# Diagonal tiles of causal attention on a packed TensorE array: the later 64 keys of a tile start 64 queries further on

## The chip, the core and the metric

The kernel runs on one core of one Trainium2 chip. A core has TensorE (PE in the profile; PEld are its weight loads), VectorE (DVE), ScalarE (ACT), GpSimd (POOL) and SyncE (SP), which issues most DMA transfers. Engines run side by side and wait for each other through semaphores. The metric is the device time of one execution in microseconds; the time before is the median of three runs.

## What is computed

The input is 4096 tokens of 256 numbers and a dense 4096 x 4096 adjacency matrix. A graph layer comes first (adjacency times features, divided by the degree, two linear maps, a residual). Then comes one transformer block in fp32: RMS norm, causal attention with 4 query heads and 2 key/value heads of 64, and a mixture of 8 experts with the 2 best per token. The part that matters here is:

```python
scores = jnp.einsum('bhtd,bhsd->bhts', q, k) / jnp.sqrt(jnp.float32(HD))
causal = jnp.tril(jnp.ones((Tx, Tx), dtype=bool))
scores = jnp.where(causal[None, None], scores, jnp.float32(-1e+30))
att = jax.nn.softmax(scores, axis=-1)
y = jnp.einsum('bhts,bhsd->bhtd', att, v)
```

A query t takes part only with keys s up to t. The order of the keys inside a sum does not matter, as long as scores and values use the same one.

## The kernel before

There are three stages: the graph layer (to about 508 us), attention with the routing of tokens to experts (508 to about 1017 us), and the experts. Queries are cut into 8 blocks of 512 (NB), keys into 32 tiles of 128 (four to a block, TB). Blocks are worked off in the order 3, 0, 4, 1, 5, 2, 6, 7 (ORDER). For each block `b` there are two passes `p`, each over one query head of either key/value head `j`; for each (b, p) the list `order_of(b)` (L795) names the key tiles `s`: all tiles of earlier blocks, then the block's own four, the diagonal ones, mixed with the last full tiles; the block's first own tile d0 comes last (for block 0 it is first, since it has no earlier tiles). There are 288 (b, p, s) in all, of which 64 are diagonal.

For one (b, p, s) the work is this.

- `scores` (L817). Keys stand on the output's partitions, queries along its columns: `ps[key, j, query]`. TensorE's 128 x 128 array is used as four quarters of 64 x 64. The product for key half `k` (HP = 64 keys) and head `j` contracts over 64 numbers, on the rows of the array that belong to `j`, and writes the partitions, so the columns of the array, that belong to `k`. On a diagonal tile `i` of its block the queries before the tile are left out: `off = i * 128`, so the four products are 512, 384, 256 or 128 wide. They are all equally wide.
- The exponential (L834) on ScalarE reads `ps` and writes a room `pt` of the ring `pt_all` (or of space lent by `res_all`, `qT_all`, `late`; `room_for_probs`, L756). On diagonal tiles GpSimd then zeroes the triangle above the diagonal in the first 128 columns (L836, a select over 128 partitions x 2 heads x 128 queries).
- `totals` (L843) on VectorE adds `pt` to the running sums, from which denominators are made later.
- `values` (L858) multiplies: the contraction is over the keys, so key half `k` sits on the rows of the array and head `j` on its columns. Half `k` sums into a bank of its own, `accs[b, p][k]` (named y_first, y_second, y_third in turn); `unload` adds the two banks.

The scores of five tiles are made ahead of values (LEAD = 5). Two PSUM buffers (`p_sc0`, `p_sc2`, in turn) take scores. The order on each engine is the order of the code (`manual_schedule`). The main loop (L1998) is:

```python
for m in range(scored, min(n + LEAD + (s == order_of(b)[0]) + 1, len(keys))):
    scores(*keys[m])
    ...
        totals(*keys[m - 1])
...
values(b, p, s)
if s == order_of(b)[-1]:
    unload(b, p)
if n % 2:
    place_for_steps(n // 2)
```

After every second tile (a place) other steps are put in, by `at` and `after` (L1132): denominators (L899), the output projection (`project`, L948), residual, routing (`choose`), `place` (L1039, which counts where each token goes in its expert's list, with 64x64 products of 32 columns at L1059) and scatters of token rows to lists in DRAM by GpSimd (L1109 copies one number of the latest `pt` into `gap`, L1110 is the indirect DMA). The products of `place` are written so:

```python
for r in range(2):
    some = slice(r * HP, (r + 1) * HP)
    for i, w in ((0, tri), (1, ones)):
        for h in range(2):
            ...
            nc.tensor.matmul(pls[r][to, i * n : (i + 1) * n], w[some, to], flat[0][some], ...)
```

Values `vv[b][key in tile, t, ...]` are written long before: for blocks 0 to 6 in `values_and_logits` of the graph stage (L636, one copy from PSUM for two tiles), for block 7 in `heads` (L256, one copy for each tile). Keys `kT[b]` hold 64 numbers of a head on partitions and keys along columns.

Of the kernel before, what the change touches and what calls it, by code (L numbers as in the profile page):

```python
# [12 lines left out]
AF = mybir.ActivationFunctionType  # L13
ALU = mybir.AluOpType
# [3 lines left out]
P = 128  # L18
# [3 lines left out]
TB = 4  # L22
NH, NKV, HD = 4, 2, 64
HEAD_ORDER = (0, 2, 1, 3)
NE = 8
# [35 lines left out]
] + list(range(NW - LAST, NW)) + list(range(NM, NG))  # L61
REG = N + SM
ROW = C + 1 + NE


@with_exitstack
def fast_kernel(
# [24 lines left out]
    nc = tc.nc  # L92
# [10 lines left out]
        out=tri, in_=tri, pattern=[[1, P]], compare_op=ALU.is_gt, fill=0.0,  # L103
        base=0, channel_multiplier=-1,
# [5 lines left out]
    for e in range(NE):  # L110
        nc.gpsimd.memset(run[0][:, e : e + 1], float(e * REG))
    lists = tc.dram_tile([NE * REG + SM, ROW], F32, name="lists")
    acc_dram = tc.dram_tile([N + SM, C], F32, name="acc_dram")
# [6 lines left out]
    for e in range(NE):  # L120
# [21 lines left out]
    qT = [  # L142
        qT_all[:, b * 1024 : (b + 1) * 1024].rearrange("p (c i) -> p c i", c=2)
        for b in range(NB)
    ]
# [34 lines left out]
    kT = [kvp.tile([P, 512], F32, name=f"kT{b}") for b in range(NB)]  # L180
    vv = [kvp.tile([P, TB, NKV * HD], F32, name=f"vv{b}") for b in range(NB)]
# [38 lines left out]
    def rotated(pool, b, t, hT, pj, ro, r2, cs, sn, unscale):  # L220
# [19 lines left out]
        nc.gpsimd.tensor_sub(ro[:, :, 0, :], ro[:, :, 0, :], r2[:, :, 0, :])  # L240
        nc.gpsimd.tensor_add(ro[:, :, 1, :], ro[:, :, 1, :], r2[:, :, 1, :])

    def heads(pool, b, t, hT, ro, tr):

        rof = ro.rearrange("p h s d -> p (h s d)")
        trf = tr.rearrange("p a b i -> p (a b) i")
        for c in range(2):
            nc.tensor.matmul(
                trf[:, 3, :], hT[:, c, t * P : (t + 1) * P], wqkv_sb[:, c, QK + NE :],
                start=(c == 0), stop=(c == 1),  # L250
            )
        for m in range(3):
            nc.tensor.transpose(trf[:, m, :], rof[:, m * P : (m + 1) * P], ident)
        nc.scalar.copy(qT[b][:, :, t * P : (t + 1) * P], trf[:, 0:2, :])
        nc.scalar.copy(kT[b][:, t * P : (t + 1) * P], trf[:, 2, :])
        nc.scalar.copy(vv[b][:, t, :], trf[:, 3, :])  # L256


    with (
# [20 lines left out]
        for h in range(2):  # L280
            some = slice(h * TB // 2, (h + 1) * TB // 2)
# [291 lines left out]
        def qkv(b):  # L573

            made = {}
# [49 lines left out]
            def values_and_logits():  # L625
                for h in range(2):
                    pj = p_tr.tile([P, 2, 2, P], F32, tag="tr", name=f"pv_{b}_{h}")
                    pj = pj.rearrange("p c t i -> p c (t i)")
                    for i in range(2):
                        at = (2 * h + i) * P  # L630
                        for c in range(2):
                            nc.tensor.matmul(  # L632
                                pj[:, i, 0 : NE + P], made["hT"][:, c, at : at + P],
                                wqkv_sb[:, c, QK:], start=(c == 0), stop=(c == 1),
                            )
                    nc.scalar.copy(vv[b][:, 2 * h : 2 * h + 2, :], pj[:, :, NE : NE + P])  # L636
                    for i in range(2):
                        t = 2 * h + i
                        nc.scalar.activation(
                            first_lg[b][:, t, :], pj[:, i, 0:NE], AF.Copy,  # L640
                            scale=made["ratio"][:, t],
                        )
# [84 lines left out]
    with (  # L727
# [14 lines left out]
        pt_all = sp.tile([P, 9 * 1024], F32, name="pt_all")  # L742
        KEPT = ROW - C
        LATE_XT = 2 * (NF + 1) * GR
# [38 lines left out]
        def next_bank():  # L783
            y_next[0] += 1
            return y_banks[(y_next[0] - 1) % 3]
# [9 lines left out]
        def order_of(b):  # L795

            whole, (d0, *part) = range(TB * b), range(TB * b, TB * b + TB)
            if not b:
                return [d0, *part]
            return [  # L800
                *whole[:-2], part[0], whole[-2], part[1], whole[-1], part[2], d0,
            ]
        HP = P // 2
        probs, sums, accs, ys, flats, chosen, squares, picks, narrows = ({} for _ in range(9))
        puts = []

# [7 lines left out]
        ]  # L814
        inverses = tc.dram_tile([2, NH, 512], F32, name="inverses")

        def scores(b, p, s):  # L817

            sb, i = divmod(s, TB)
            off = i * P if sb == b else 0  # L820
            w = 512 - off
            ps = next(p_sa).tile([P, 2, 512], F32, tag="sc", name=f"sc_{b}_{p}_{s}")
            for k in range(2):
                for j in range(2):
                    hd = slice(j * HD, (j + 1) * HD)
                    nc.tensor.matmul(  # L826
                        ps[k * HP : (k + 1) * HP, j, :w],
                        kT[sb][hd, i * P + k * HP : i * P + (k + 1) * HP], qT[b][hd, p, off:],
                        start=True, stop=True,
                    )  # L830
            room = room_for_probs()
            room_of[id(room)] = b, p, s
            pt = room.rearrange("p (j i) -> p j i", j=2)
            nc.scalar.activation(pt[:, :, :w], ps[:, :, :w], AF.Exp, scale=HD ** -0.5)  # L834
            if sb == b:
                nc.gpsimd.affine_select(  # L836
                    out=pt[:, :, 0:P], in_=pt[:, :, 0:P], pattern=[[0, 2], [1, P]],
                    compare_op=ALU.is_ge, fill=0.0, base=0, channel_multiplier=-1,
                )
            probs[b, p, s] = pt  # L840
            latest[:] = [pt]

# [15 lines left out]
        def values(b, p, s):  # L858
            sb, i = divmod(s, TB)
            off = i * P if sb == b else 0  # L860
            pt = probs.pop((b, p, s))
            if s == order_of(b)[0]:
                accs[b, p] = next_bank(), next_bank()
            for k in range(2):
                some = slice(k * HP, (k + 1) * HP)
                for j in range(2):
                    hd = slice(j * HD, (j + 1) * HD)
                    nc.tensor.matmul(  # L868
                        accs[b, p][k][hd, off:], vv[sb][some, i, hd], pt[some, j, : 512 - off],
                        start=(s == order_of(b)[0]), stop=(s == order_of(b)[-1]),  # L870
                    )

        def unload(b, p):
            ys[b, p] = ax.tile([P, 512], F32, tag=f"yT{p}", name=f"yT_{b}_{p}")
# [58 lines left out]
        def inputs(b):  # L933

            row = ax.tile([P, TB, ROW], F32, tag="row", name=f"row_{b}")
            for t in range(TB):
# [53 lines left out]
        def over(v):  # L990
            return v.to_broadcast([P, TB, NE])
# [47 lines left out]
        def place(b):  # L1039
# [12 lines left out]
            else:  # L1052
                pls = two_banks(f"pl_{b}")
# [4 lines that stand above are left out]
                            to = slice(h * HP, (h + 1) * HP)  # L1058
                            nc.tensor.matmul(  # L1059
# [21 lines left out]
            nc.vector.tensor_add(oh1, oh1, oh2)  # L1081
            nc.vector.tensor_mul(row[:, :, C + 1 : ROW], oh1, over(den))
            chosen[b] = slots
# [97 lines left out]
        def last_qkv():  # L1181
# [4 lines left out]
            def norm():  # L1186
                h0 = ax.tile([P, TB, ROW], F32, tag="row", name="h0_l")
                for t in range(TB):
                    nc.vector.tensor_scalar(
                        in_order(h0[:, t, 0:C]), in_groups(res[b][:, t, :]),  # L1190
                        mv[b][:, t, 0:1], both[b][:, t], op0=ALU.subtract, op1=ALU.mult,
                    )
                made["ratio"] = ratio(ax, b)
                nc.sync.dma_start(
                    turning_l.rearrange("(t p) c -> p t c", p=P), h0[:, :, 0:C]
                )
# [98 lines left out]

        pad = eg.tile([P, ROW], F32, name="pad")
        nc.gpsimd.memset(pad, 0.0)
# [5 lines left out]
        def step_iota(name, n, first, step):  # L1303
# [1522 lines left out]
```

## Time and profile before

| | us |
|---|---|
| three runs | 1511.27, 1512.95, 1515.51 |
| their median | 1512.95 |
| the profiled execution's own time | 1511.47 |
| its span, from first to last instruction | 1509.8 |
| attention stage | 508 to 1017 |
| TensorE busy over the span | 1496.9 (99%) |
| VectorE, ScalarE, GpSimd busy | 1083.9, 544.9, 568.9 |
| granted TensorE clock | 0.999 |

A line of a group reads: code line, engine, operation, output<-inputs, shapes (partitions x elements; 64*64 is the part of the array in use), count, busy us, mean ns of one, idle time before and what ended it. A line of a timeline begins with the start and the duration in us. Matmuls are pipelined, and their ends are modelled, so starts say more than durations.

### The profile page before, as it was taken

The numbers are of one execution on the slowest core, as the hardware profiler recorded it, in microseconds if no ns is written. First come the engines' busy times: TensorE is split into PE (matmuls) and PEld (weight loads), VectorE is DVE, ScalarE is ACT, GpSimd is POOL, SyncE is SP. The second block draws the span as 40 slices with busy tenths as digits, with TensorE's granted clock in tenths as the row PEclk, the third lists the DMA queues.
The fourth block names the chain that finished last, engine by engine and source line by source line (L and its number), as shares of the span: only waits on it lengthen the run. The fifth ranks groups of instructions, "written<-read, shape, count | busy, mean of one in ns | idle before, by whom it ended". The sixth has DMA issues, their size and how long they took to land. (4 is left out here: it accounts for less than half of the span.)

```text
span 1509.8 us, 28585 instructions
## 1 busy us (share of the span) xinstructions
PE 1496.9 (99%) x10731; PEld 1102.8 (73%) x10731; DVE 1083.9 (72%) x2239; ACT 544.9 (36%) x975; POOL 568.9 (38%) x649
## 2 busy tenths in 40 slices
PE   9999999999999999999999999999999999999997
PEld 7888888888888544444444444358899999999996
DVE  7855666656765577779879879795676877777872
ACT  2102011021020455655665655653222334343341
POOL 2102122121221331374565553551523464554542
PEclk9999999999999999999999999999999999999999
DMA  7435645555566000011010110029977898999965
GB/s 244 133 119 178 201 147 173 166 170 171 162 184 185 21 15 22 24 59 30 30 59 28 36 41 30 30 87 336 251 180 225 254 278 233 264 272 246 270 155 135
DMA packets 127005, 220.56 MB, mean 146 GB/s; under 512 B 79530, under 2 KB 103338, under 8 KB 113226
## 3 DMA queue, kind: packets, MB, share of 16 engines
q1 hardware_dynamic: 113322, 200.39, 42.3%
q0 software_dynamic: 12720, 17.47, 6.6%
q8 instruction: 86, 1.41, 0.4%
q10 hardware_dynamic: 816, 0.79, 0.2%
q14 instruction: 61, 0.50, 0.1%
HBM read 188.67 MB, written 31.33 MB: 146 GB/s over the span
## 5 line engine op out<-in xcount | busy, mean ns | idle before, releaser
L826 PE MATMUL sc<-qT_all,kT 64*64 64x512 f32 (+3 forms) x2304 | 282.1, 557 | 0.5 <-ACT pt_all L834 0.3
L538 PE MATMUL acc<-a,g 128*128 128x256 f32 x1024 | 244.0, 379 | 0.0
L538 PEld LDWEIGHTS acc<-a,g 128*128 128x128 f32 x1024 | 194.1, 190 | 32.2 <-issue 6.7
L826 PEld LDWEIGHTS sc<-qT_all,kT 64*64 64x64 f32 x2304 | 91.3, 133 | 128.9 <-issue 109.9
L834 ACT ACTIVATE pt_all<-sc 128x1024 f32<-128x1024 f32 (+3 forms) x157 | 149.0, 956 | 99.9 <-PE sc L826 95.6
L1917 POOL DMA_INDIRECT acc_dram<-y,late x40 | 63.3, 1583 | 177.0 <-ACT y L1906 118.9
L538 PE MATMUL acc<-more_sums,g 128*128 128x256 f32 x512 | 126.3, 379 | 0.0
L854 DVE TENSOR_TENSOR late<-late,pt_all 128x1024 f32<-128x1024 f32 (+3 forms) x92 | 106.6, 1159 | 20.4 <-ACT pt_all L834 9.0
L661 POOL TENSOR_TENSOR rot<-rot,tables 128x512 f32<-128x512 f32 x21 | 34.4, 1636 | 192.4 <-ACT rot L657 137.3
L538 PEld LDWEIGHTS acc<-more_sums,g 128*128 128x128 f32 x512 | 97.2, 190 | 13.2
L868 PE MATMUL y_second<-pt_all,vv 64*64 64x512 f32 (+3 forms) x440 | 105.0, 555 | 0.0
L868 PE MATMUL y_first<-pt_all,vv 64*64 64x512 f32 (+3 forms) x440 | 104.3, 553 | 0.0
L1837 PE MATMUL h<-late,qT_all 128*128 128x256 f32 (+1 forms) x616 | 104.0, 327 | 0.0
L1837 PEld LDWEIGHTS h<-late,qT_all 128*128 128x128 f32 x616 | 93.5, 191 | 9.6 <-ACT late L1521 0.8
L1110 POOL DMA_INDIRECT lists<-row,slots x64 | 91.3, 1426 | 17.2 <-issue 14.5
L636 ACT COPY vv<-pv 128x256 f32<-128x256 f32 x14 | 5.2, 373 | 251.9 <-PE pv L632 216.0
L868 PE MATMUL y_third<-pt_all,vv 64*64 64x512 f32 (+3 forms) x376 | 89.8, 557 | 0.0
L1844 DVE TENSOR_TENSOR late<-si,h 128x256 f32<-128x256 f32 (+2 forms) x87 | 39.3, 466 | 64.4 <-ACT si L1843 44.6
L657 ACT ACTIVATE rot<-pq 32x512 f32<-32x512 f32 x84 | 49.5, 589 | 82.5 <-DVE qT_all L655 33.1
L1843 ACT ACTIVATE si<-h 128x256 f32<-128x256 f32 (+2 forms) x87 | 36.1, 418 | 107.0 <-PE h L1837 93.1
L538 PE MATMUL acc<-qT_all,g 128*128 128x256 f32 x256 | 65.7, 379 | 0.0
L854 DVE TENSOR_TENSOR sum_all<-sum_all,pt_all 128x1024 f32<-128x1024 f32 (+3 forms) x49 | 53.5, 1093 | 15.8 <-POOL pt_all L836 9.9
(480 smaller groups left out, 3321.4 us busy)
## 6 DMA issues: line engine op xcount, KB each, us to landing
a<-in_adj_dram SPq DMA_DIRECT2D x64, 1024.0 KB
qT_all<-in_w_dram SPq DMA_DIRECT2D x18, 1408.0 KB
pt_all<-in_w_dram SPq DMA_DIRECT2D x16, 1408.0 KB
res_all<-in_w_dram SPq DMA_DIRECT2D x17, 768.0 KB
pt_all<-in_w_dram SPq DMA_DIRECT2D x16, 768.0 KB
res_all<-in_w_dram SPq DMA_DIRECT2D x8, 1408.0 KB
qT_all<-in_w_dram SPq DMA_DIRECT2D x9, 768.0 KB
late<-lists SPq DMA_DIRECT2D x96, 64.0 KB
```

What stands on the lines that cost most here:

```text
L538: nc.tensor.matmul(acc[bank][:, at, :], g[jb][:, right, k, :], m[left][:, k, :], start=(jb == 0 and k == 0 and at == 0), stop=(jb == NB - ...
L657: nc.scalar.activation(rot[n * Q : (n + 1) * Q, :], pj[(n ^ 1) * Q : ((n ^ 1) + 1) * Q, :], AF.Copy, scale=1.0 if n % 2 else -1.0,)
L661: nc.gpsimd.tensor_mul(rot, rot, tables[b][:, 1, :])
L826: nc.tensor.matmul(ps[k * HP : (k + 1) * HP, j, :w], kT[sb][hd, i * P + k * HP : i * P + (k + 1) * HP], qT[b][hd, p, off:], start=True, st ...
L834: nc.scalar.activation(pt[:, :, :w], ps[:, :, :w], AF.Exp, scale=HD ** -0.5)
L854: nc.vector.tensor_add(sums[b, p][:, :, off:], before[:, :, off:], pt[:, :, : 512 - off])
L868: nc.tensor.matmul(accs[b, p][k][hd, off:], vv[sb][some, i, hd], pt[some, j, : 512 - off], start=(s == order_of(b)[0]), stop=(s == order_o ...
L1110: put = nc.gpsimd.indirect_dma_start(out=lists[:, :], out_offset=bass.IndirectOffsetOnAxis(ap=chosen[b][:, k, t, :], axis=0), in_=flats[b] ...
L1837: nc.tensor.matmul(ps[m % 2][:, m // 2 - q, :], w13_sb[:, c, m * P : (m + 1) * P], xT[:, c, :], start=(c == 0), stop=(c == 1),)
L1843: nc.scalar.activation(si[:, 0:both, :], ps[0][:, 0:both, :], AF.Silu)
L1844: nc.vector.tensor_mul(hT[:, q : q + both, :], si[:, 0:both, :], ps[1][:, 0:both, :])
L1917: put = nc.gpsimd.indirect_dma_start(out=(acc_dram if k < NM - LAST else out)[:, :], out_offset=at, in_=y[:, h, :], in_offset=None, comput ...
```

## The change

On a diagonal tile, the first 64 queries of the tile see only its first 64 keys. The change leaves out the products of the later 64 keys with these queries.

- `narrowed(b, s)` gives, for each key half k of the layout, how many query columns are skipped: 64 for the half that holds the later keys, 0 for the other. `scores` and `values` start their products that much further on. In `values` the first tile of a sum (only block 0's d0 is diagonal there) is left whole.
- In odd tiles the halves are swapped: k = 0 holds the later 64 keys. `key_half(t, k)` picks the columns of `kT` for it, and `value_rows` writes the rows of `vv` in this order. For that, one copy of two tiles becomes one copy for the even tile and two copies of 64 rows for the odd tile; in `heads` one copy becomes two on odd tiles.
- The exponential of a diagonal tile runs on all 128 partitions from column 64 on; a second one takes columns 0 to 63 of the early half's 64 partitions. GpSimd zeroes the triangle in the early half (64 partitions, columns 0 to 63), sets columns 0 to 63 of the late half to 0 (memset), and zeroes the triangle in the late half (columns 64 to 127): three instructions for one. `totals` stays as it is.

```diff
+def key_half(t, k):
+    return slice((k ^ t % 2) * HP, ((k ^ t % 2) + 1) * HP)
...
+    def value_rows(b, t, made):
+        if t % 2 == 0:
+            nc.scalar.copy(vv[b][:, t, :], made)
+        else:
+            for k in range(2):
+                nc.scalar.copy(vv[b][k * HP : (k + 1) * HP, t, :], made[key_half(t, k)])
...
-        nc.scalar.copy(vv[b][:, t, :], trf[:, 3, :])
+        value_rows(b, t, trf[:, 3, :])
...
-                    nc.scalar.copy(vv[b][:, 2 * h : 2 * h + 2, :], pj[:, :, NE : NE + P])
+                    for i in range(2):
+                        value_rows(b, 2 * h + i, pj[:, i, NE : NE + P])
...
+        quarters = [(k, j) for k in range(2) for j in range(2)]
+        def narrowed(b, s):
+            if s // TB != b:
+                return 0, 0
+            late_half = 1 - s % 2
+            return tuple(HP if k == late_half else 0 for k in range(2))
...
+            skips = narrowed(b, s)
+            for k, j in quarters:
+                hd = slice(j * HD, (j + 1) * HD)
+                nc.tensor.matmul(
+                    ps[k * HP : (k + 1) * HP, j, skips[k] : w],
+                    kT[sb][hd, i * P :][:, key_half(i, k)], qT[b][hd, p, off + skips[k] :],
+                    start=True, stop=True,
+                )
...
-            nc.scalar.activation(pt[:, :, :w], ps[:, :, :w], AF.Exp, scale=HD ** -0.5)
+            begin = max(skips)
+            nc.scalar.activation(
+                pt[:, :, begin:w], ps[:, :, begin:w], AF.Exp, scale=HD ** -0.5
+            )
             if sb == b:
-                nc.gpsimd.affine_select(
-                    out=pt[:, :, 0:P], in_=pt[:, :, 0:P], pattern=[[0, 2], [1, P]],
-                    compare_op=ALU.is_ge, fill=0.0, base=0, channel_multiplier=-1,
-                )
+                early = skips.index(0)
+                for k in (early, 1 - early):
+                    some, cols = slice(k * HP, (k + 1) * HP), slice(skips[k], skips[k] + HP)
+                    if k == early:
+                        nc.scalar.activation(
+                            pt[some, :, cols], ps[some, :, cols], AF.Exp, scale=HD ** -0.5
+                        )
+                    else:
+                        nc.gpsimd.memset(pt[some, :, 0:HP], 0.0)
+                    nc.gpsimd.affine_select(
+                        out=pt[some, :, cols], in_=pt[some, :, cols], pattern=[[0, 2], [1, HP]],
+                        compare_op=ALU.is_ge, fill=0.0, base=0, channel_multiplier=-1,
+                    )
...
+            skips = narrowed(b, s) if s != order_of(b)[0] else (0, 0)
+            for k, j in quarters:
+                some, hd = slice(k * HP, (k + 1) * HP), slice(j * HD, (j + 1) * HD)
+                nc.tensor.matmul(
+                    accs[b, p][k][hd, off + skips[k] :], vv[sb][some, i, hd],
+                    pt[some, j, skips[k] : 512 - off],
+                    start=(s == order_of(b)[0]), stop=(s == order_of(b)[-1]),
+                )
```

More of the change, by code (lines that the diff above doesn't have):

```diff
@@ L63 @@
 ROW = C + 1 + NE
+HP = P // 2
+def key_half(t, k):
+    return slice((k ^ t % 2) * HP, ((k ^ t % 2) + 1) * HP)
 @with_exitstack
@@ L802, in order_of @@
             ]
-        HP = P // 2
         probs, sums, accs, ys, flats, chosen, squares, picks, narrows = ({} for _ in range(9))
@@ L822, in scores @@
             ps = next(p_sa).tile([P, 2, 512], F32, tag="sc", name=f"sc_{b}_{p}_{s}")
[L823 to L829, printed above, removed]
-                    )
+            skips = narrowed(b, s)
[6 more added lines that the diff above has]
+                )
             room = room_for_probs()
@@ L833, in scores @@
             pt = room.rearrange("p (j i) -> p j i", j=2)
-            nc.scalar.activation(pt[:, :, :w], ps[:, :, :w], AF.Exp, scale=HD ** -0.5)
+            begin = max(skips)
+            nc.scalar.activation(
+                pt[:, :, begin:w], ps[:, :, begin:w], AF.Exp, scale=HD ** -0.5
+            )
             if sb == b:
-                nc.gpsimd.affine_select(
-                    out=pt[:, :, 0:P], in_=pt[:, :, 0:P], pattern=[[0, 2], [1, P]],
-                    compare_op=ALU.is_ge, fill=0.0, base=0, channel_multiplier=-1,
-                )
+                early = skips.index(0)
[11 more added lines that the diff above has]
+                    )
             probs[b, p, s] = pt
@@ L863, in values @@
                 accs[b, p] = next_bank(), next_bank()
[L864 to L871, printed above, removed]
+            skips = narrowed(b, s) if s != order_of(b)[0] else (0, 0)
[6 more added lines that the diff above has]
+                )
         def unload(b, p):
```

## The prediction, made before the result was known

> **What bounds the kernel now.** I read the stretches first, then single instructions of TensorE in order of time, then the groups by shape, then the timeline of GpSimd. The change touches the attention stage, from 508 to 1017 us. In the table of stretches (busy us of each engine, granted clock, DMA share) it reads:
>
> ```profile
> core 0: us, PE busy (x) PEld busy (x) DVE busy (x) ACT busy (x) POOL busy (x), PEclk, DMA share, GB/s
> 508.00:1017.00 509.00, 508.49 (x4935) 217.98 (x4931) 415.94 (x733) 300.99 (x392) 243.88 (x282) 1.00 0.12 37
> ```
>
> TensorE never stops, VectorE has 93 us to spare, ScalarE 208, GpSimd 265, and DMA is nearly idle. A busy PE with modelled ends proves little, so I look at starts. Each fp32 product is recorded twice (2304 records for 288 tiles of four products in scores): I call one record a pass. The timeline around a tile of 384 queries, and around one of 128:
>
> ```profile
> 525.39 0.59 PE L868 MATMUL y_first<-pt_all,vv 64*64 64x512 f32 x1
> ...
> 525.82 0.82 PE L826 MATMUL sc<-qT_all,kT 64*64 64x384 f32 x8
> 526.47 0.59 PE L868 MATMUL y_first<-pt_all,vv 64*64 64x512 f32 x1
> ...
> 657.11 0.27 PE L868 MATMUL y_second<-late,vv 64*64 64x128 f32 x1
> ...
> 657.22 0.27 PE L868 MATMUL y_second<-late,vv 64*64 64x128 f32 x1
> ...
> 657.33 0.61 PE L826 MATMUL sc<-qT_all,kT 64*64 64x256 f32 x8
> ```
>
> What to see: four passes of 64x64 start within some 20 ns, one on each quarter of the array, and the next four 0.43 us later for 512 columns, 0.65/2 for 384 (525.82 to 526.47) and 0.11 for 128. To the nanosecond the starts are 429, 322, 216 and 109 apart for 512, 384, 256 and 128 columns: 53.4 ns for 64 columns, with no wait between tiles. Over the stage starts leave this rhythm only where the shape on the array changes (denominators, L948 and the like, about 0.1 us before and after). So a column fewer on every quarter is time off the end, and the expert stage after it runs gapless too (100.00 busy of 100 from 1200 to 1300), so nothing there takes it back unless transfers do.
>
> **Does a quarter gain by itself?** The change shortens two of four quarters at a time. Before, all four always have equal widths, so the trace doesn't show this case directly. The nearest row is the small products of `place` (L1059), written in the code as all of r=0 (into pl), then all of r=1 (into y_first):
>
> ```profile
> 635.36 0.20 PE L1059 MATMUL pl<-r_took,tri 64*64 64x32 f32 x2
> 635.38 0.25 PE L1059 MATMUL y_first<-r_took,tri 64*64 64x32 f32 x2
> ...
> 635.52 0.22 PE L1059 MATMUL pl<-r_took,ones 64*64 64x32 f32 x1
> ...
> 635.56 0.62 PE L826 MATMUL sc<-qT_all,kT 64*64 64x512 f32 x1
> 635.57 0.22 PE L1059 MATMUL y_first<-r_took,ones 64*64 64x32 f32 x1
> ```
>
> y_first, eight passes later in the code, starts before most of pl; and a score product starts at 635.56 while a product of y_first that stands before it in the code starts at 635.57. Each quarter works off its own queue; afterwards the two halves keep a lead of 57 ns through all widths. The Trainium skill speaks against this: "TensorE: Matmul & The Clock Gate", Part 3 "The mechanism", under what overlaps, has matmuls starting and ending strictly in program order. Taken so that a quarter can't run ahead, a set of four lasts as long as its widest pass, two full quarters hide two narrow ones, and the sum of the change is 0. By the row it is the full saving. I go by the row, since it is from this kernel's own stage, and keep 0 as the other end: the lead it shows is 57 ns, and the change needs up to about 214 (two products of two passes).
>
> **The sum on TensorE.** For each of 16 pairs (b, p) there are four diagonal tiles. Scores put the key half k on column half k of the array, values on row half k. Even tiles narrow k=1, odd ones k=0 (that is what the swap does), so each quarter is narrow in two of four tiles in scores and two in values: 4 products, 8 passes, 8 x 53.4 = 427 ns. Tiles of 128 go to 64 columns: the linear value is 56 ns a pass, while the 32-column passes of L1059 repeat at 58, so weight loading may set 58: 109 - 58 = 51 ns saved. That costs 5 to 10 ns a pair. 16 x 0.42 = 6.7 us. Tile 0 of block 0 stays whole in values (it opens the sum): 2 x 107 ns off two quarters, 6.6 left for the slowest. At a change of shape all quarters wait for the last, and a lead standing there is lost; such places fall mostly between the clusters, 0.1. **TensorE: -6.5 us.** Without the swap the second key half alone would gain and the first would set the pace: 0.
>
> **ScalarE.** By-shape groups of the exponential (busy us, mean ns):
>
> ```profile
> L834 ACT ACTIVATE pt_all<-sc 128x1024 f32<-128x1024 f32 x130 | 132.2, 1024 | 94.3 <-PE sc L826 90.4 <-DVE row L937 1.3 <-DVE late L854 1.1
> ...
> L834 ACT ACTIVATE pt_all<-sc 128x512 f32<-128x512 f32 x9 | 5.4, 596 | 1.8 <-PE sc L826 1.8
> ...
> L834 ACT ACTIVATE pt_all<-sc 128x256 f32<-128x256 f32 x7 | 2.7, 382 | 0.3
> ```
>
> 428 ns for 512 elements: 0.84 each over a fixed 168. The main exponential loses 128 elements, -107 ns; the added one on 64 rows of 128 elements costs 168 + 107 = 275. Net +168 ns, 64 times, 10.8 us. It is covered: scores of tile n+2 need this bank, and on diagonal tiles they start 0.23 us (block 0) or later, mostly 1 to 1.7 us, after the exponential's end. Where the cover is 0.23, the shorter scores (-0.1) and +0.17 use it just up: at most 0.1. The value copies: 14 of 373 ns (128x256) become 14 of 128x128 (283 measured at L256) and 28 of 64 rows, +28 instructions, some +0.5 us a step of L636, in a stage where ScalarE is busy 76 of 500 us and the banks are next asked for a step later: 0. `heads` adds two copies of the same kind behind the key copies in the attention stage: 0. No step moves and no DMA is added, so SP's queue stays as it is.
>
> **GpSimd.** A select of 128x256 becomes two selects of 64x128 and a memset of 64x128, in this order: early half, memset, late half. The rows near it:
>
> ```profile
> L836 POOL TENSOR_SCALAR_AFFINE_SELECT pt_all<-pt_all 128x256 f32<-128x256 f32 x36 | 21.8, 608 | 102.1 <-ACT pt_all L834 74.6 <-DVE late L854 27.1 <-issue 0.2
> ...
> L1109 POOL COPY gap<-pt_all 128x1 f32<-128x1 f32 x24 | 13.5, 563 | 30.7 <-DVE r_cand L1075 18.8 <-ACT pt_all L834 11.2
> ```
>
> The select is 0.40 at its quickest, 1.45 at its slowest; the copy of one element 0.18 to 1.07, mean 0.56. So an instruction costs its presence more than its size. From below, each of the three takes 0.25: +0.35 a tile. From above 0.56 each, against 0.61: +1.1. I take +0.9, nearer the copy, because both run beside the same VectorE adds: 64 x 0.9 = 58 us on an engine with 265 free. Behind these stand the scatter's gap copy and lists (L1109, L1110), 2 us a place, which had to wait for a later tile's exponential anyway. Who waits: VectorE's totals (in about 28 of 64 tiles they start at once when the select ends; elsewhere VectorE is 1 to 6 us behind and notices nothing), and the values five tiles on. VectorE idles 93 us and loses at most 28 x 1.2 = 34; it feeds TensorE at L948, where the tightest cover is 2.4 us (block 6's normalized y, no diagonal tile near) and else over 4. Values start 1.9 us or more after their select, median about 6. The tightest:
>
> ```profile
> 1016.16 0.50 POOL L836 TENSOR_SCALAR_AFFINE_SELECT res_all<-res_all 128x256 f32<-128x256 f32 x1 [1.91 <-ACT res_all L834]
> ...
> 1018.54 0.60 PE L868 MATMUL y_first<-res_all,vv 64*64 64x512 f32 x2
> ```
>
> New chain there: +0.17 of ScalarE, +0.9, leaves 0.8. With delays adding up over a cluster of four, one or two of the 64 may stall: 0 to 1 us, I take **+0.3**.
>
> **Sum.** -6.5 + 0.3 = -6.2. The profiled execution took 1511.47 us with a span of 1509.8 (1.7 around it), so 1503.6 of span and 1505.3; the median of the runs is 1.5 above that execution, so 1512.95 - 6.2 = **1506.7 us**, 0.41% faster. About 0.3% (4.5 us) is what a measurement of this kernel tells from no change.
>
> **Rivals.** (1) *Quarters go in step*, or the lead stops at some 57 ns: for it the skill's rule, against it L1059. 0 to -3 us: 1510 to 1513. In the same place ends a gain that the experts' weights take back, at a DMA share of 0.80 to 0.93 there; against that, TensorE shows no wait for them, and the loads are released by the attention stage's own instructions, so they move with it. (2) *GpSimd becomes what values wait for.* Place: L868 on a diagonal tile behind the last select. If all three instructions take the slowest select's 1.45, the chain grows by some 4 us; the seven tiles with covers of 1.9 to 3.9 us (19.6 together) then lack 7 x 4 - 19.6 = 8 us, and queues on GpSimd stretch others: +8 to +12 less 6.5, 1514 to 1519. It decides from about 3 us of growth a tile. Against: one op in the timeline rarely meets a slow neighbour three times. (3) *ScalarE holds the scores*: if +168 ns came through whole on the 8 diagonal tiles with cover under 1 us, +1.3, so 1508.0; for it that only two sc banks turn, against it the covers.
>
> **Chances.** Forecast 0.6 (its own range 1505 to 1508.5); no or part gain 0.21; ScalarE eats a part 0.07; GpSimd 0.12. Faster by over 0.3% (under 1508.4): 0.55 of the forecast and 0.05 of ScalarE's case, 0.6. Slower by over 0.3% (above 1517.5): only the worse end of GpSimd's and unseen stalls, 0.1. Within: 0.3. The range 1504 to 1514 leaves out the worse part of GpSimd's case and a tenth at most besides.
>
> **What would show it.** Right: passes of one quarter 53 ns shorter on diagonal tiles, with the two halves drifting apart by 100 to 200 ns and meeting again, the stage 6 to 6.6 us shorter, the experts' stage as long as before. Wrong: sets of four spaced by their widest pass (then the gain is 0); PE waits for L836's successors; sc waiting for the added exponential; exposed DMA after 1010.

## The result and the profile after

The changed kernel takes **1531.67 us** (median of 4 runs, 1530.74 to 1533.48), against 1512.12 us for the kernel before in the same series: a ratio of 1.0133, 95% interval 1.0121 to 1.0145. It is 1.3% slower. The forecast was 1506.7, faster, with a range of 1504 to 1514, so it was wrong in sign and in size. The profiled execution took 1531.82 us with a span of 1530.1, 20.3 more than before.

First the table of stretches of the changed kernel (busy us of each engine with the number of instructions, granted clock of TensorE, DMA share, GB/s):

```profile
core 0: us, PE busy (x) PEld busy (x) DVE busy (x) ACT busy (x) POOL busy (x), PEclk, DMA share, GB/s
508.00:1017.00 509.00, 495.02 (x4735) 246.03 (x4731) 397.57 (x698) 297.66 (x440) 261.33 (x386) 0.99 0.10 32
640.00:800.00 160.00, 149.14 (x1392) 83.27 (x1388) 116.93 (x211) 85.40 (x133) 95.94 (x138) 0.96 0.11 35
...
650.00:660.00 10.00, 8.25 (x76) 4.35 (x72) 2.60 (x5) 2.69 (x4) 5.84 (x12) 1.00 0.09 30
660.00:670.00 10.00, 7.25 (x46) 2.44 (x46) 6.96 (x11) 4.51 (x11) 6.77 (x12) 0.66 0.08 28
...
1200.00:1300.00 100.00, 100.00 (x825) 97.98 (x825) 79.61 (x192) 39.21 (x100) 52.14 (x55) 1.00 0.92 263
```

and, for comparison, 640 to 800 us of the kernel before:

```profile
640.00:800.00 160.00, 160.00 (x1600) 70.27 (x1596) 130.30 (x236) 96.08 (x129) 92.15 (x104) 1.00 0.13 42
```

TensorE had half a microsecond of gaps in the whole stage before; now it idles for 14 us, and 10.9 of these lie between 640 and 800 us. VectorE and ScalarE are less busy there than before, and GpSimd, at 95.9 of 160 us (92.2 before), is far from full: no engine has become a bound, they wait for each other. The experts' stage is gapless as before, and the stage's beginning hasn't moved (first scores at 507.75 against 507.78 us).

The waits from 508 to 1038 us (engine, what and where it was, what it waited for: us in total, times, longest) say for what:

```profile
POOL pt_all L871 <- DMA lists<-row,slots: 18.0, 12, 2.9
DVE late L889 <- POOL pt_all L871: 17.1, 8, 4.7
...
ACT qT_all L1015 <- DVE row L989: 14.0, 3, 5.9
...
POOL res_all L871 <- DMA lists<-row,slots: 7.2, 3, 4.1
...
PE sc L849 <- ACT pt_all L858: 6.0, 5, 2.8
...
POOL qT_all L871 <- DMA lists<-row,slots: 4.1, 1, 4.1
...
POOL late L871 <- DMA lists<-row,slots: 3.5, 3, 1.8
```

L871 is the select of a diagonal tile. Nineteen of the 128 selects wait, 32.8 us together, for `lists<-row,slots`: the landing of the indirect DMA with which GpSimd scatters token rows (L1145, the L1110 of before). Before the change no select had that releaser (the prediction's line of L836 names what ended its idle time).

The trace also names the semaphores that each instruction waits for. In the kernel before, the landings of the 56 scatters of this stage are waited for on GpSimd only by 48 later scatters. In the changed kernel each of the 56 is waited for once, by a select that begins on partition 64 or by a wait instruction of L871 just ahead of it. So the wait stands in the compiled program; it is not a delay inside the engine.

The other lines are the way on: `totals` (L889) wait for the select, ScalarE's squares (L1015) wait for the residual (L989) that stands behind `totals` on VectorE, and scores wait for the exponentials that stand behind the squares on ScalarE. Once, in order of time (start, duration, engine, line, with idle time before and its releaser in brackets):

```profile
656.77 1.05 POOL L1145 DMA_INDIRECT lists<-row,slots  x1 [0.16 <-issue]
...
657.84 0.30 POOL L871 TENSOR_SCALAR_AFFINE_SELECT pt_all<-pt_all 64x128 f32<-64x128 f32 x1
...
658.20 0.20 POOL L870 MEMSET pt_all<- 64x128 f32 x1
659.59 0.29 POOL L871 TENSOR_SCALAR_AFFINE_SELECT pt_all<-pt_all 64x128 f32<-64x128 f32 x1 [1.18 <-DMA lists<-row,slots]
659.91 1.22 DVE L889 TENSOR_TENSOR late<-late,pt_all 128x1024 f32<-128x1024 f32 x1 [2.97 <-POOL pt_all L871]
...
661.06 0.41 DVE L989 TENSOR_TENSOR row<-row,po 128x256 f32<-128x256 f32 x1
...
661.50 0.42 ACT L1015 ACTIVATE qT_all<-row 128x256 f32<-128x256 f32 x1 [5.93 <-DVE row L989]
...
662.58 1.41 ACT L858 ACTIVATE pt_all<-sc 128x1024 f32<-128x1024 f32 x2
...
663.65 2.20 PE L849 MATMUL sc<-qT_all,kT 64*64 64x512 f32 x14 [2.75 <-ACT pt_all L858]
...
665.63 1.06 PE L902 MATMUL y_first<-res_all,vv 64*64 64x512 f32 x1
...
666.48 1.06 PE L902 MATMUL y_first<-res_all,vv 64*64 64x512 f32 x1
```

The even tile's first select (partitions 0 to 63) and its memset follow the issue of the scatter at once. The second select, on partitions 64 to 127, stands still until 659.59. From there the delay runs through VectorE and ScalarE into TensorE. The last two lines show a second loss: products of 512 columns now start 0.85 us apart where they had started 0.43 apart. TensorE works at half its clock there, and once more near 786 us, as the granted clock (after the bracketed counts) tells:

```profile
661.80:663.60 1.80, 0.00 (x0) 0.00 (x0) 1.28 (x3) 1.75 (x6) 0.55 (x1) 0.50 0.21 75
663.60:668.40 4.80, 4.75 (x30) 2.15 (x32) 2.78 (x3) 2.47 (x7) 3.27 (x7) 0.50 0.08 30
668.70:680.00 11.30, 11.30 (x116) 6.80 (x112) 4.74 (x9) 5.38 (x10) 7.74 (x13) 1.00 0.09 26
...
784.60:791.30 6.70, 5.22 (x28) 2.53 (x32) 6.39 (x6) 4.82 (x8) 4.57 (x5) 0.50 0.17 61
```

TensorE is busy for 4.75 + 5.22 us at half rate, which loses about 5 us (an estimate from these rows). The added idle time (13.5) and the half rate (5) do not make up all that was lost, which is the 21.1 us of the next table and the gain of about 4: some 6 us are not traced here one by one. A part of them is time in which one half of the array stands still while the other works, which counts as busy: half `k` = 0 of a tile's values starts at 658.20, half `k` = 1, behind the late select, at 659.93.

This is how much later the last values of a pass start than before, in us, by the starts in the traces (minus is earlier). The experiments of the next section stand beside the change. The shift that is there when the stage begins is not taken off: -0.27 in e10, +0.23 in e3, within 0.07 in the others.

```
end of (b, p)   change     e1     e10     e3      e8
(3, 1)          -0.71    -0.66   -0.77   +0.23   +0.04
(0, 1)          -0.58    -0.61   -0.82   +0.23   +0.03
(4, 0)          -0.80    -0.82   -1.10   +0.23   +0.03
(4, 1)          +2.16    -1.29   -1.46   +0.23   +3.38
(1, 1)          +8.97    -0.74   -1.25   +1.32  +10.08
(5, 1)         +13.00    -1.44   -1.89   +1.32  +11.95
(2, 1)         +17.65    -2.20   -2.65   +1.32  +16.38
(6, 1)         +19.89    -3.04   -3.49   +1.32  +16.38
(7, 1)         +21.08    -3.89   -4.34   +1.32  +18.35
```

Up to (4, 0), which ends near 625 us, the change gains 0.8 us. The first scatter is issued at 645 us; everything is lost after it.

### The profile page after: what moved, and what is told of

It reads as the page before. It is cut to its first block, busy times and chain, and to the rows that moved or that the text cites. A ratio compares the mean times of both kernels' runs of the same rounds, so it can differ in the third digit from the quotient of the medians.

```text
span 1530.1 us, 28950 instructions
## 1 busy us (share of the span) xinstructions
PE 1504.7 (98%) x10731; PEld 1143.2 (75%) x10731; DVE 1082.0 (71%) x2239; ACT 560.0 (37%) x1069; POOL 605.7 (40%) x777
## 5 line engine op out<-in xcount | busy, mean ns | idle before, releaser
L849 PE MATMUL sc<-qT_all,kT 64*64 64x512 f32 (+7 forms) x2304 | 293.1, 557 | 7.9 <-ACT pt_all L858 6.0
L849 PEld LDWEIGHTS sc<-qT_all,kT 64*64 64x64 f32 x2304 | 110.5, 134 | 120.3 <-issue 85.6
L858 ACT ACTIVATE pt_all<-sc 128x1024 f32<-128x1024 f32 (+4 forms) x157 | 145.2, 932 | 93.9 <-PE sc L849 87.0
L889 DVE TENSOR_TENSOR late<-late,pt_all 128x1024 f32<-128x1024 f32 (+3 forms) x92 | 106.8, 1161 | 29.6 <-POOL pt_all L871 17.1
L902 PE MATMUL y_second<-pt_all,vv 64*64 64x512 f32 (+5 forms) x440 | 106.9, 549 | 2.7 <-POOL pt_all L871 2.7
L1145 POOL DMA_INDIRECT lists<-row,slots x64 | 97.5, 1524 | 24.4 <-DVE row L1117 12.9
L902 PE MATMUL y_first<-pt_all,vv 64*64 64x512 f32 (+6 forms) x440 | 106.1, 549 | 0.0
L252 ACT COPY vv<-pv 128x128 f32<-128x128 f32 x14 | 3.7, 267 | 250.4 <-PE pv L646 143.9
L902 PE MATMUL y_third<-pt_all,vv 64*64 64x512 f32 (+7 forms) x376 | 91.4, 553 | 1.3 <-POOL pt_all L871 0.7
L871 POOL TENSOR_SCALAR_AFFINE_SELECT pt_all<-pt_all 64x128 f32<-64x128 f32 x72 | 35.7, 498 | 100.4 <-ACT pt_all L866 53.9
L889 DVE TENSOR_TENSOR sum_all<-sum_all,pt_all 128x1024 f32<-128x1024 f32 (+3 forms) x49 | 53.8, 1097 | 19.7 <-POOL pt_all L871 12.6
```

The source lines that it names most:

```text
L849: nc.tensor.matmul(ps[k * HP : (k + 1) * HP, j, skips[k] : w], kT[sb][hd, i * P :][:, key_half(i, k)], qT[b][hd, p, off + skips[k] :], sta ...
L858: nc.scalar.activation(pt[:, :, begin:w], ps[:, :, begin:w], AF.Exp, scale=HD ** -0.5)
L871: nc.gpsimd.affine_select(out=pt[some, :, cols], in_=pt[some, :, cols], pattern=[[0, 2], [1, HP]], compare_op=ALU.is_ge, fill=0.0, base=0, ...
L889: nc.vector.tensor_add(sums[b, p][:, :, off:], before[:, :, off:], pt[:, :, : 512 - off])
L902: nc.tensor.matmul(accs[b, p][k][hd, off + skips[k] :], vv[sb][some, i, hd], pt[some, j, skips[k] : 512 - off], start=(s == order_of(b)[0] ...
L1145: put = nc.gpsimd.indirect_dma_start(out=lists[:, :], out_offset=bass.IndirectOffsetOnAxis(ap=chosen[b][:, k, t, :], axis=0), in_=flats[b] ...
```

## The experiments

Theory 1, the wait: a select that begins on partition 64 waits for the scatters in flight. Theory 2, the count: three GpSimd instructions in place of one delay by their number. Theory 3: TensorE's part gains nothing anyway.

**e1_low: the change, with no select beginning on partition 64.**

```diff
+                nc.gpsimd.memset(pt[(1 - early) * HP : (2 - early) * HP, :, 0:HP], 0.0)
...
-                    else:
-                        nc.gpsimd.memset(pt[some, :, 0:HP], 0.0)
+                    low = slice(0, (k + 1) * HP)
                     nc.gpsimd.affine_select(
-                        out=pt[some, :, cols], in_=pt[some, :, cols], pattern=[[0, 2], [1, HP]],
-                        compare_op=ALU.is_ge, fill=0.0, base=0, channel_multiplier=-1,
+                        out=pt[low, :, cols], in_=pt[low, :, cols], pattern=[[0, 2], [1, HP]],
+                        compare_op=ALU.is_ge, fill=0.0, base=k * HP, channel_multiplier=-1,
```

> The changed kernel with the same three GpSimd instructions for a diagonal tile, but no select begins on partition 64: where it did, the select takes all 128 partitions of the same 64 columns, with a base under which the lower 64 are kept. (The memset stands first, so that all of what the select reads is written.) Theory 1, the wait: a select that begins on partition 64 waits for the scatters in flight, and this wait costs some 26 us, of which TensorE's saving of 6.5 is taken off. Then e1 takes 1505 to 1508, no select shows lists as its releaser, and TensorE is gapless over the stage. Theory 2, the count: three GpSimd instructions in place of one hold GpSimd, VectorE and so the rooms, whatever they wait for. Then e1 stays at 1527 to 1535. Theory 3, TensorE's part gains nothing: even with the wait gone it ends at 1512 to 1513.

Measured: **1507.16 us** (1506.78 to 1507.76), ratio to before 0.9955, interval 0.9938 to 0.9971. Its stretches:

```profile
508.00:1017.00 509.00, 507.83 (x4965) 258.50 (x4962) 419.67 (x737) 311.56 (x462) 273.01 (x411) 1.00 0.12 38
640.00:800.00 160.00, 159.58 (x1612) 91.29 (x1607) 130.41 (x239) 99.56 (x158) 103.97 (x159) 1.00 0.13 42
```

TensorE's gaps are gone, the clock stays at 1.00, and no select waits for lists. The number and kind of GpSimd instructions are those of the change; only the partitions of one select of each tile differ, and the place of the memset. This run shows what the change gains and costs without the wait. In its trace the landings of the scatters are again waited for by 48 later scatters alone. So theory 1 holds, theories 2 and 3 don't.

**e2_rows, e3_three and e8_copy: the kernel before, with only its select edited or a copy added.** In e2 the select is made as two by partitions, in e3 as two by columns with a memset of partitions 64 to 127 between them, and in e8 a copy of partitions 64 to 127 follows it:

```diff
 e2
-                    out=pt[:, :, 0:P], in_=pt[:, :, 0:P], pattern=[[0, 2], [1, P]],
+                for k in range(2):
+                    some = slice(k * HP, (k + 1) * HP)
...
+                        out=pt[some, :, 0:P], in_=pt[some, :, 0:P], pattern=[[0, 2], [1, P]],
+                        compare_op=ALU.is_ge, fill=0.0, base=-k * HP, channel_multiplier=-1,
...
 e3
+                for k in range(2):
+                    if k:
+                        nc.gpsimd.memset(pt[HP:, :, 0:HP], 0.0)
+                    cols = slice(k * HP, (k + 1) * HP)
...
+                        out=pt[:, :, cols], in_=pt[:, :, cols], pattern=[[0, 2], [1, HP]],
+                        compare_op=ALU.is_ge, fill=0.0, base=k * HP, channel_multiplier=-1,
...
 e8
+                nc.gpsimd.tensor_copy(pt[HP:, :, 0:HP], pt[HP:, :, 0:HP])
```

> The kernel before with one edit: the select of a diagonal tile is made as two, partitions 0 to 63 and 64 to 127, over all 128 columns each. Nothing is narrowed and nothing swapped. Theory 1, the wait: the second one stands still for the scatters, so 1530 to 1542 (the 1512 of before plus up to the 26 that the wait cost), with releasers named lists on its line. Theory 2, the count: one instruction more where the change had two more, so some 1520 to 1526, with no such releaser.

> The kernel before with one edit: the select of a diagonal tile becomes three GpSimd instructions, a select of columns 0 to 63 on all 128 partitions, a memset of partitions 64 to 127 in these columns, and a select of columns 64 to 127 on all 128 partitions. Theory 1, the wait: no select begins on partition 64, so 1512 to 1514, GpSimd's added time is hidden. Theory 2, the count: as slow against before as the change without its saving on TensorE, 1530 to 1538.

> The kernel before with one instruction added on GpSimd behind each select of a diagonal tile: a copy of partitions 64 to 127, columns 0 to 63, onto themselves. It asks whether the wait belongs to the select or to any GpSimd instruction that reads from partition 64 on. If to any: the copy waits for the scatters in flight, releasers named lists stand on its line, and the time is as in e2, 1528 to 1540. If to the select alone: one instruction more, which e3 showed to be hidden, 1511 to 1514.

Measured: e2 **1535.07 us** (ratio 1.0145, 1.0126 to 1.0163), e8 **1531.19 us** (1.0116, 1.0101 to 1.0132), e3 **1510.98 us** (0.9981, 0.9972 to 0.9989). GpSimd's waits in e2:

```profile
POOL pt_all L838 <- DMA lists<-row,slots: 15.3, 11, 3.1
...
POOL res_all L838 <- DMA lists<-row,slots: 6.0, 4, 2.4
...
POOL late L838 <- DMA lists<-row,slots: 3.6, 3, 1.2
...
POOL qT_all L838 <- DMA lists<-row,slots: 1.9, 1, 1.9
```

and in e8, where L840 is the copy:

```profile
POOL pt_all L840 <- DMA lists<-row,slots: 13.3, 12, 1.7
...
POOL late L840 <- DMA lists<-row,slots: 6.5, 4, 2.7
...
POOL res_all L840 <- DMA lists<-row,slots: 2.8, 3, 1.4
...
POOL qT_all L840 <- DMA lists<-row,slots: 1.9, 1, 1.9
```

Two selects, each on half the partitions, cost 22 us together and the added copy 19; three instructions by columns cost nothing that the times show. Nothing is narrowed or swapped in these kernels, so the wait makes the loss, and it belongs to the copy as well as to the select. Selects and copies of all 128 partitions, selects of partitions 0 to 63 and the memset of 64 to 127 don't wait. The scatter neither reads nor writes what the select and the copy work on, so no data asks for this wait. In these two traces each of the 56 scatters is waited for once by e2's selects and by e8's copies, in e3 by 48 later scatters alone: the compiled programs differ in it. Why the wait is put there, and whether the chip needs it, no run here shows.

e3's median is a little under that of before. Its profiled execution is not: its span is 1510.9 against 1509.8, and one stall of 1.1 us lies ahead of block 1. Its waits from 648 to 664 us:

```profile
DVE late L858 <- POOL pt_all L840: 1.9, 1, 1.9
...
ACT qT_all L984 <- DVE row L958: 1.2, 1, 1.2
...
PE sc L826 <- ACT pt_all L834: 0.9, 1, 0.9
```

This is the same way through VectorE, residual and ScalarE, here from longer GpSimd work alone. The count has a price, once, 1.1 us.

**e4_fewer: as e1, with one select (even tiles) or two (odd ones) beside the memset.**

```diff
+                if early == 0:
...
+                        out=pt[:, :, 0:P], in_=pt[:, :, 0:P], pattern=[[0, 2], [1, P]],
...
+                else:
...
+                        out=pt[0:HP, :, HP:P], in_=pt[0:HP, :, HP:P], pattern=[[0, 2], [1, HP]],
...
+                        out=pt[:, :, 0:HP], in_=pt[:, :, 0:HP], pattern=[[0, 2], [1, HP]],
```

> The changed kernel with fewer GpSimd instructions and none of its selects beginning on partition 64: memset of the late half first; on even tiles then one select of 128 partitions and 128 columns as before the change, on odd tiles two (partitions 0 to 63 in columns 64 to 127, and all partitions in columns 0 to 63). Theory 1, the wait: 1505 to 1508, like e1 within 1 us. Theory 2, the count: two or three instructions in place of one, so between before and after, 1515 to 1530, and under e1.

Measured: 1508.1 us (ratio 0.9965, 0.995 to 0.9979), within 1 us of e1, as theory 1 had it. Fewer instructions gain nothing over e1; the 1515 to 1530 of theory 2 are far off.

**e5_noswap: e1 without the swap of the halves.**

```diff
-    return slice((k ^ t % 2) * HP, ((k ^ t % 2) + 1) * HP)
+    return slice(k * HP, (k + 1) * HP)
...
-            late_half = 1 - s % 2
+            late_half = 1
```

> e1 without the swap: k = 1 holds the later 64 keys in every tile, and value rows are copied as before the change. The same number of passes is shortened by the same amounts, but always on the quarters of k = 1. Independent quarters: those of k = 0 keep their full width and set the pace, TensorE's saving is 0, and the second exponential costs the 2 us that blocks 0 and 1 lose in e1, so 1511 to 1515, and the start of k = 1's products runs ahead of k = 0's within a cluster of diagonal tiles until k = 0 stops it. Strict program order or a set of four that lasts as long as its widest pass: 0 as well, but then e1 could not have gained either. A pace set by the sum of the columns: as fast as e1, 1506 to 1508.

Measured: 1510.69 us (ratio 0.9989, 0.9982 to 0.9996), just under the 1511 to 1515 of independent quarters; last values 0.64 us earlier than before where e1 has 3.89. The timeline of its TensorE in block 7, before a diagonal tile, after one and after two:

```profile
951.40 0.59 PE L902 MATMUL y_second<-pt_all,vv 64*64 64x512 f32 x1
...
951.41 0.59 PE L902 MATMUL y_second<-pt_all,vv 64*64 64x512 f32 x1
...
952.26 0.81 PE L849 MATMUL sc<-qT_all,kT 64*64 64x384 f32 x8
952.81 0.59 PE L902 MATMUL y_second<-pt_all,vv 64*64 64x512 f32 x1
...
952.90 0.59 PE L902 MATMUL y_second<-pt_all,vv 64*64 64x512 f32 x1
...
955.39 0.69 PE L849 MATMUL sc<-qT_all,kT 64*64 64x192 f32 x8
955.71 0.59 PE L902 MATMUL y_second<-qT_all,vv 64*64 64x512 f32 x1
...
955.91 0.59 PE L902 MATMUL y_second<-qT_all,vv 64*64 64x512 f32 x1
```

Two quarters that had started 10 ns apart start 0.09 apart behind the first narrowed scores and 0.20 behind the second: each quarter runs as its own products allow. The one that is never narrowed sets the pace, and nearly nothing is gained. A pace set by the sum of columns would have given e1's time. The 0.04 a pass that it does gain is not explained. Though the second exponential is in it, neither block 0 nor block 1 loses over 0.05 us in this kernel, whose scores come hardly earlier.

**e7_values and e9_scores: e1 with the scores, or the values, of all diagonal tiles left whole.** The edits are `skips = narrowed(b, s) if b < 0 else (0, 0)` in `scores` (so never narrowed) with the selects that this needs (one on even tiles; on odd ones partitions 0 to 63 over all 128 columns, and all partitions over columns 0 to 63), and `skips = 0, 0` in `values`.

> e1 with the values narrowed and the scores of all diagonal tiles whole: one exponential, no memset, one select on even tiles and two on odd ones. Half of TensorE's saving, 16 pairs of 0.21, less tile 0 of block 0: 3.1 us, with nothing added on ScalarE: 1509 to 1510.5. If the second exponential costs more than the half that the scores save, e7 is as fast as e1 or faster.

> e1 with the scores narrowed and the values of all diagonal tiles whole. Half of TensorE's saving, 3.4 us, less what the second exponential takes back in blocks 0 and 1 (some 2 us): 1510.5 to 1512.5. If the scores' narrowing is worth as much as the values', 1509 to 1510.5 as in e7.

Measured: e7 1510.05 us (0.9983, 0.9976 to 0.999), e9 1509.56 us (0.9977, 0.9969 to 0.9986). In blocks 6 and 7 each pass gains 0.20 to 0.21 us in either kernel, and 0.41 to 0.43 in e1. Scores and values are worth the same there. By the medians e9's second expectation holds; by the profiled executions the scores' half is worth less over the stage (last values 1.19 us earlier, 2.07 in e7, of which 0.18 was there as its stage began), since e9 loses 1.1 us in block 1, where e1, e6 and e7 lose less.

**e6_short_full and e10_later: where the rest of the gain stays.** e6 is e1 with whole scores in blocks 0 and 1; e10 is e1 with these blocks left altogether as before the change, their keys not swapped.

```diff
 e6
-            skips = narrowed(b, s)
+            skips = narrowed(b, s) if b > 1 else (0, 0)
...
 e10
-            if s // TB != b:
+            if s // TB != b or b < 2:
                 return 0, 0
...
+            if sb == b and b < 2:
+                nc.gpsimd.affine_select(
+                    out=pt[:, :, 0:P], in_=pt[:, :, 0:P], pattern=[[0, 2], [1, P]],
```

> e1, but in blocks 0 and 1 (4 and 8 key tiles for a pass p, so nearly all or half of them diagonal) the scores are left whole: one exponential, no memset, one select on even tiles and two on odd ones; values stay narrowed. Theory: of the 6.5 us that TensorE should save, e1's trace shows 3.9 by the end of the stage; the pairs of blocks 2, 6 and 7 save 0.42 to 0.43 each as forecast, and the four pairs of blocks 0 and 1, which should save 1.7, are 0.4 later at their end, since scores wait for the second exponential there. Then with whole scores these four pairs save the values' part, 0.6 to 0.8, so 1 us less than e1: 1505.5 to 1507 (by the trace's starts: 0.6 to 0.8 earlier over them). Rival: what these blocks lose has to do with the unequal quarters or with GpSimd; then they stay about 0.4 later, 1506.5 to 1508.

> e1 with blocks 0 and 1 left as before the change, scores, exponential, select and values whole and their keys not swapped; blocks 2 to 7 as in e1. In e1's trace the four pairs of blocks 0 and 1 end 0.6 us later than before, where they should have saved 1.7; the other twelve save 4.5. If that loss comes from what the change does on these blocks' own tiles (the second exponential at pass 1 of block 1, the longer GpSimd sequence at pass 0), it is gone: about 0.6 less than e1, last values 4.3 to 4.6 earlier than before, 1506 to 1507. If it comes from block 4's tiles, whose GpSimd work stands just ahead of block 1, pass 0 of block 1 loses 0.8 to 1.1 here too, and it ends as e1 does: last values 3.4 to 3.9 earlier, 1507 to 1508.

Measured: e6 1507.25 us (0.9962, 0.9948 to 0.9975), e10 **1506.74 us** (0.9962, 0.9949 to 0.9976). The shift of the last values over each pass, in us:

```
            e1      e6      e10
(0, 0)    +0.08   -0.11   -0.05
(1, 0)    +0.22   +0.83   +0.21
(1, 1)    +0.33   -0.13    0.00
```

My theory for e6 was that these blocks lose because scores wait for the second exponential. At (1, 1) and a little at (0, 0) that fits: with whole scores the loss is gone (though e6 has less GpSimd work on these tiles too, so the exponential is not shown alone). At (1, 0) it is wrong, and the time lies where the rival had it: with one exponential e6 loses more. e3 loses 1.09 at the same place, so the GpSimd work just ahead, of block 4's tiles, takes part in it. ScalarE's squares don't explain the rest: their one wait for the residual in e1 (1.9 us) comes after 690 us, that of e10 near block 1 is 0.2 us, and both lose 0.2 at (1, 0). This stays open. For e10 the first expectation is the nearer: 1506.74 us, (1, 1) free of its loss, (1, 0) not made worse. But its stage began 0.27 us earlier, so it gained 4.1 within the stage where e1 gained 3.9, less than the 0.6 more that I expected. e10 is the fastest run of the study, and not measurably faster than e1.

## Why the prediction was wrong, point by point

**The bound: right.** In e1, without the new wait, TensorE is busy 507.83 of 509 us and the experts' stage passes the shift on.

**Quarters gain by themselves: right.** The row of `place` that I went by held; in e5's lines the lead grows to 0.20 us without a stop. The rule of the Trainium skill that was weighed there ("TensorE: Matmul & The Clock Gate", Part 3 "The mechanism", strict program order) would have given 0, and by e1, e5 and the half gains of e7 and e9 it doesn't hold for quarters.

**TensorE's sum of -6.5: right in its unit, too large in its total.** 0.42 a pass (b, p) was the forecast (its total has a slip: 6.7 less twice 0.107 leaves 6.5, not 6.6, which decides nothing); blocks 6 and 7 show 0.41 to 0.43. Over the stage e1 gains 3.9: blocks 2 to 7 give 4.5, mostly what they should, and blocks 0 and 1 take 0.6 back where they should have given 1.7. Whole times say 6.0 by the medians, spans 4.4.

**ScalarE: sizes right, the cover nearly.** 275 ns for the added exponential were 266; the main one of 896 elements took 918 ns where 0.84 each over 168 makes 921. "At most 0.1" became about 0.5 us in block 1, by the difference of e1 and e6 at (1, 1); that scores came earlier there while the exponential came later is the likely reason, and not shown alone. The value copies cost nothing, as the beginning of the stage shows.

**GpSimd: here it failed.** These are the groups by shape of e1, which has the same three instructions without the wait (busy us, mean ns):

```profile
L871 POOL TENSOR_SCALAR_AFFINE_SELECT pt_all<-pt_all 64x128 f32<-64x128 f32 x36 | 20.1, 558 | 4.8 <-ACT pt_all L867 3.9
...
L871 POOL TENSOR_SCALAR_AFFINE_SELECT pt_all<-pt_all 128x128 f32<-128x128 f32 x36 | 17.1, 475 | 72.8 <-ACT pt_all L867 63.7 <-issue 7.8 <-POOL pt_all L863 0.7
...
L863 POOL MEMSET pt_all<- 64x128 f32 x36 | 7.3, 203 | 15.3 <-PE y_first L902 10.0 <-PE y_third L902 4.3
```

558 + 475 + 203 = 1236 ns for 608 before, on the 36 tiles in `pt_all`: +0.63 a tile, inside the bounds of 0.35 to 1.1 and under the +0.9 taken. So the durations were no mistake. The step that failed is the one that made GpSimd's part +0.3 us: it put a new wait of the selects at nothing. "Behind these stand the scatter's gap copy and lists", it says, "which had to wait for a later tile's exponential anyway", and, further up, "No step moves and no DMA is added". It looked at what stands behind the selects and at how long they take, and never asked what they stand behind. An edit that puts a GpSimd instruction on other partitions added a wait for a DMA that was there all along. Nineteen such waits, 32.8 us on GpSimd, turned the gain of some 4 us by the last values into a loss of 21.1.

A second step failed with it: that a late VectorE matters to TensorE only at L948, with a cover of 2.4 us or more. The way that was taken is another one: `totals`, residual, ScalarE's squares, the exponentials behind them, scores. The squares waited 14.0 us in three places for the residual in the changed kernel, 1.9 in e1. Before the change that line was in the waits with 0.4 us, and I passed over it:

```profile
ACT qT_all L980 <- DVE row L954: 0.4, 1, 0.4
```

**The rivals.** The second, "GpSimd becomes what values wait for", named the engine, but priced it by slow selects and set it at 1514 to 1519. What came has another cause and another size: L871's wait, not its duration, and e3 shows that durations alone cost 1.1 us. The first rival is denied by e1, the third was right for half a microsecond of block 1 at most.

## What to carry to other kernels

Price an added or reshaped instruction by three things: its duration, what stands behind it, and what it must wait for. On an engine that also issues DMAs, give the third as much care as the first; in this kernel, selects and copies on GpSimd that began on partition 64 were compiled with a wait for the scatters in flight, those that began on partition 0 were not, and a mask over all 128 partitions with a shifted base did the same work for no wait. When a change loses where it should gain, look in the lists of waits for a releaser that wasn't there before: here an edit of a few lines made 1507.16 us of 1531.67.

## What was not expected of the hardware

- GpSimd instructions that read from partition 64 on (a select of 64x128 or 64x256, a copy of 64x128) waited for indirect DMAs in flight, 1.7 us on average in the changed kernel and up to 4.1. A memset of the same partitions didn't. The waits are semaphores in the compiled program; that the hardware itself would hold these instructions is not shown.
- Stalls took the clock with them. TensorE idled for 2.75 us up to 663.65 and for 2.62 us up to 786.08, each time with shorter gaps in the microseconds before. The granted clock was at 0.50 from 661.8 and from 784.6 us at the latest, about 1 us into these gaps, and stayed there for over 6.6 us (to 668.4 and 791.3). The Trainium skill ("TensorE: Matmul & The Clock Gate", Part 1, "What's actually happening") has the half rate set in after an idle window of about 3.4 us and end after about as long under load; here no single gap was that long, and TensorE was busy at half rate for 4.75 and 5.22 us. In e1, where no wait of scores for an exponential exceeds 0.3 us, the granted clock is 1.00 over the stage.
- Quarters of the array with products of unequal width drifted apart by 0.20 us in e5's lines, and those ahead were not held back until they were even.
